# Layer 3's weight products placed behind layer 2's experts, and the first expert's matrices issued ahead of its rows

## The chip, the cores and the metric

The kernel runs on one core of one Trainium2 chip. The metric is the time of one execution on the device, in microseconds (us). Five engines work side by side, each through its own queue of instructions in order: TensorE (PE), VectorE (DVE), ScalarE (ACT), GpSimd (POOL) and SyncE (SP). SP and ACT also issue plain DMA transfers, POOL the indirect ones.

## The reference, cut to what matters

The program is a stack of four hybrid layers on an image of 256 channels and 64 x 64 pixels. Layers 0 and 1 are convolutional. Layers 2 and 3 work on 4096 tokens of 256 numbers; each is an attention and then a mixture of 8 experts, of which each token uses the two that its router ranks highest:

```python
def _L2_ffn_ref(input_embeddings, router_w, w1, b1, w2, b2):      # hidden size 256
    ...
            logits = tokens.astype(jnp.float32) @ router_w.astype(jnp.float32).T
            probs = jax.nn.softmax(logits, axis=-1)
            rw, re = jax.lax.top_k(probs, TOP_K)
    ...
            for e in range(E):
                h = jax.nn.gelu(tokens @ w1[e] + b1[e], approximate=False)
                y = h @ w2[e] + b2[e]
                out = out + combine[:, e:e + 1] * y
def _L3_attn_ref(x, Wq, bq, Wk, bk, Wv, bv):
    Q = jnp.einsum('bsd,de->bse', x, Wq) + bq
    K = ...
    V = jnp.einsum('bsd,de->bse', x, Wv) + bv
    scores = jnp.einsum('bqd,bkd->bqk', Q, K) * scale
    weights = jax.nn.softmax(scores, axis=-1)
    return jnp.einsum('bqk,bkd->bqd', weights, V)
def _L3_ffn_ref(x, Wg, bg, W1, b1, W2, b2):                       # hidden size 1024
    ...
        out = out + w_dense[:, e:e + 1] * (h @ W2[e] + b2[e])

t = _to_tokens(x)
t = t + _L2_attn_ref(_ln_t(t), ...)
t = t + _L2_ffn_ref(_ln_t(t), ...)
t = t + _L3_attn_ref(_ln_t(t), ...)
t = t + _L3_ffn_ref(_ln_t(t), ...)
```

## The kernel before, in words

The tokens stay in one SBUF array `t`, 128 partitions by 32 tiles of 256. `run` (L2465) calls `attn2`, `attn3`, `experts` and `store` in turn, each layer's expert stage in three steps:

- `route` (L1771) takes a block of four tiles. It normalizes the tokens into `n` (for layer 2 it also writes the normalized tokens, added to `t`, back into `t`: L1783, and four activations on ACT, L1785), turns `n` over on PE in two halves (k = 0 is copied by ACT, k = 1 by DVE, L1792), multiplies by the router's matrix, picks the best two experts (`top2`), counts how many rows each expert has so far, and writes every token's row to its expert's place in the DRAM array `xs` by eight indirect scatters on POOL (L1828). It is a generator: the attention's loop runs it piece by piece between its own blocks, and the last of the eight blocks is routed after the attention's end. In layer 2 `n` lies in attention's array `a_qk`, in layer 3 in `f_room`.
- `tile_table` (L1835) works out on DVE, from the counts, which expert each tile of 256 rows belongs to and at which row of `xs` it starts. It ends in the table `tab`, from which SP reads a register for the expert (row 0 of the table) and one for the first row (row 1).
- `experts` (L1889) runs `expert_tiles` (L1906) over 36 tiles, and over three more only if they are needed. `load(i)` reads the two registers and issues three DMAs on SP: the rows `f_x` (L1919, 260 KB), and the expert's matrices `f_w1` (L1921) and `f_w2` (L1923), together 0.65 MB in layer 2 and 2.2 MB in layer 3. Loads run three tiles ahead in layer 2, two in layer 3. `turn` (L1926) turns the rows over on PE and copies them to `f_xT` on DVE (L1932). `first` (L1936) multiplies by `w1` and applies Gelu on ACT (L1942). `where` (L1945) is nine DVE operations on two numbers per partition (L1950 to L1958) that find where each row's result goes and its weight. In layer 3 `sides` combines parts of `w2` on POOL into `f_wt` (L1969), and `seven` (L1972) forms the second product from seven smaller ones, with sums `f_hs` of DVE. `second` (L2001) scatters the results to the DRAM array `ys` by two indirect scatters on POOL (L2012).

Layer 3's attention needs three matrices that are products of its weights: `wvp` (one subtraction on DVE, L2119), `wqk` (PE, copied at L2124) and `bqk` (PE, copied at L2127). `attn3` (L2092) loads the weights for them into a pool of their own, `weights3` (three DMAs, L124, two on SP and one on ACT's queue), computes the products, and only then calls `self.experts(S)` for layer 2:

```python
self.weights(wpool, ["w_qkT3", "w_v3p", "w_v3s"])
nc.vector.tensor_tensor(wvp, w["w_v3p"], w["w_v3s"], ALU.subtract)
...
self.experts(S)
```

After that, its `add(b)` (L2144) fetches two results per token from `ys` (`outputs`, L2040) and adds them to `t` on DVE (L2151), and the attention starts.

The library's scheduler orders each engine's instructions by a model of their times and may move one ahead of others that were written earlier. Inside `tc.manual_schedule(engines=...)` the named engines keep the written order: PE in layer 2's attention loop, PE and POOL in layer 3's, whose `tile_table` is in the same block. Buffers come from pools; a pool that opens on memory which an earlier one used makes its writers wait for the earlier use to end.

Of the kernel before, what the change touches and what calls it, by code (L numbers as in the profile page):

```python
# [10 lines left out]
F32 = mybir.dt.float32  # L11
BF16 = mybir.dt.bfloat16
I32 = mybir.dt.int32
AF = mybir.ActivationFunctionType
ALU = mybir.AluOpType
# [73 lines left out]
class Net:  # L89
# [1088 lines left out]
    def attn2(self, t, S):  # L1178

        nc, tc = self.nc, self.tc  # L1180
        with tc.tile_pool(name="a2", bufs=1) as pool:
            A = {}
            A["qk"] = pool.tile([P, NT, 2 * C], F32, tag="qk", name="a2_qk")
            A["v"] = pool.tile([P, NT, C], F32, tag="v", name="a2_v")
            A["vT"] = pool.tile([P, 2, N], F32, tag="vT", name="a2_vT")

            for nm in ("sim", "gate", "fac"):
                A[nm] = pool.tile([P, 2, NT // 2, NH], F32, tag=nm, name=f"a2_{nm}")
            wg_bd = pool.tile([P, 2, P], F32, tag="wg_bd", name="wg_bd")
            self.kv_blocks(pool, None, wg_bd)  # L1190

            ked = pool.tile([P, 2, D], F32, tag="ked", name="a2_ked")
            nc.sync.dma_start(out=ked, in_=self.A["kvn_ed"].rearrange("(m p d) -> p m d", p=P, d=D))
            dif = pool.tile([P, 2, D], F32, tag="dif", name="a2_dif")
            nc.vector.tensor_tensor(dif, ked, bc(ked[:, :, 0], 2, D), ALU.not_equal)
            nc.vector.tensor_reduce(self.flags[:, 1:2], dif.rearrange("p m d -> p (m d)"), AX.X, ALU.max)
            with (
                tc.tile_pool(name="a2w", bufs=2) as wp,
                tc.tile_pool(name="a2_ps", bufs=2, space=PSUM) as ps,
            ):  # L1200
                self.rows(wp, "b_qkv2", "b_qkv2")


                stages = [self.attn2_project(b, t, A, wg_bd, wp, ps) for b in range(NBLK)]
                go = lambda b, *names: [stages[b][nm]() for nm in names if 0 <= b < NBLK]
                with tc.manual_schedule(engines={mybir.EngineType.PE}):
                    go(0, "norm", "turn")
                    for b in range(-1, NBLK):
                        go(b + 2, "norm")
                        go(b + 1, 0)  # L1210
                        go(b, "turn_v", "lengths")
                        go(b + 1, 1, 2)
                        go(b, "sims")
                        go(b + 1, 3)
                        go(b + 2, "turn")
                        go(b, "gates")
            self.attn2_fac(A)
            with (
                tc.tile_pool(name="a2x", bufs=2) as wp,
                tc.tile_pool(name="a2x_ps", bufs=1, space=PSUM) as ps,  # L1220
            ):
                bank = lambda: ps.tile([P, NB], F32, tag="r", name="f_r_ps")

                def route(t0, T):

                    n = A["qk"][:, t0 : t0 + T, :].rearrange("p t c -> p (t c)")[:, : T * CX]
                    nT = A["v"][:, t0 : t0 + T, :].rearrange("p t c -> p (t c)").rearrange("p (a n) -> p a n", a=2)
                    return self.route(t0, T, t, S, wp, n.rearrange("p (i c) -> p i c", c=CX), nT, bank)

                self.attn2_sum(t, A, ked, wp, ps, route)  # L1230
            with (
                tc.tile_pool(name="a2t", bufs=1) as wp,
                tc.tile_pool(name="a2t_ps", bufs=1, space=PSUM) as ps,
            ):
                self.tile_table(S, wp, lambda: ps.tile([P, NB], F32, tag="r", name="f_r_ps"))

    def kv_blocks(self, pool, kv_bd, wg_bd):

# [532 lines left out]
    def route(self, t0, T, t, S, wp, n, nT, bank):  # L1771
# [6 lines left out]
        small = lambda p: p[:, : T * NE].rearrange("p (i e) -> p i e", e=NE)  # L1778
        flat = lambda a: a.rearrange("p i e -> p (i e)")
        r, shift = self.layer_norm(wp, t[:, tiles, :], n[:, :, :C], 1e-5, on_act=(L == 2))  # L1780
        if L == 2:

            nc.vector.tensor_scalar_add(r, r, 1.0)  # L1783
            for i in range(T):
                nc.scalar.activation(t[:, t0 + i, :], t[:, t0 + i, :], AF.Identity, bias=shift[:, i : i + 1], scale=r[:, i : i + 1])  # L1785
        nc.gpsimd.tensor_copy(n[:, :, C], self.out_row[:, tiles])
        yield
        for k in range(2):
# [1 line left out]
            for i in range(T):  # L1790
                nc.tensor.transpose(p[:, i * P : (i + 1) * P], n[:, i, k * P : (k + 1) * P], self.ident)
            (nc.scalar.copy, nc.vector.tensor_copy)[k](nT[:, k, :], p[:, : T * P])  # L1792
            yield
        p = small(bank())
        for i in range(T):
            self.mm(p[:, i, :], [(nT[:, kt, i * P : (i + 1) * P], wr[:, kt, :]) for kt in range(2)])
# [37 lines left out]
    def tile_table(self, S, wp, bank):  # L1834
# [6 lines left out]

        ci = tl([NE], "ci", I32)
        nc.vector.tensor_copy(ci, c_ps)
        rows = tl([NE], "rows")
        nc.vector.tensor_copy(rows, c_ps)
        nc.vector.tensor_single_scalar(ci, ci, MT - 1, ALU.add)
        nc.vector.tensor_single_scalar(ci, ci, MT.bit_length() - 1, ALU.arith_shift_right)
        cnt = tl([NE], "cnt")
        nc.vector.tensor_copy(cnt, ci)
        ends = tl([NE], "ends")  # L1850
        nc.vector.tensor_copy(ends[:, 0:1], cnt[:, 0:1])
        for e in range(1, NE):
            nc.vector.tensor_add(ends[:, e : e + 1], ends[:, e - 1 : e], cnt[:, e : e + 1])

        last = tl([1], "last")
        nc.vector.tensor_scalar_add(last, ends[:, NE - 1 : NE], -1.0)
# [3 lines left out]
        nc.vector.tensor_tensor(past, bc(ends, 1, NTILE), bc(tau, 2, NE), ALU.is_le)  # L1860
        ex = S["ex"]
        nc.vector.tensor_reduce(ex, past, AX.X, ALU.add)
        nc.vector.tensor_tensor(past, past, bc(cnt, 1, NTILE), ALU.mult)
        skip = tl([NTILE], "skip")
        nc.vector.tensor_reduce(skip, past, AX.X, ALU.add)
        nc.vector.tensor_sub(tau, tau, skip)
        nc.vector.tensor_scalar_mul(tau, tau, float(MT))
        nc.vector.scalar_tensor_tensor(skip, ex, float(N), tau, ALU.mult, ALU.add)
        tab = S["tab"]
        nc.vector.tensor_scalar_mul(tab[:, 0, :], ex, float(P))  # L1870
        nc.vector.tensor_copy(tab[:, 1, :], skip)
        nc.vector.tensor_copy(S["used"], ends[:, NE - 1 : NE])

        nc.vector.tensor_tensor(past, bc(ex, 2, NE), bc(self.count[:, :NE], 1, NTILE), ALU.is_equal)
# [30 lines left out]
    def expert_tiles(self, S, tiles, wp, ps):  # L1905
# [7 lines left out]
        def load(i):  # L1913
# [2 lines left out]
            row = nc.values_load(tab[0:1, 1, i : i + 1], engines=[mybir.EngineType.SP], min_val=0, max_val=NE * N - MT,  # L1916
                                 skip_runtime_bounds_check_because=why)
            x = wp.tile([P, NI, CX], F32, tag="x", name="f_x", bufs=ahead + 3)
            nc.sync.dma_start(out=x, in_=self.xs[bass.ds(row, MT), :].rearrange("(i p) c -> p i c", p=P))  # L1919
            w1 = wp.tile([P, 2 * hidden + KH], F32, tag="w1", name="f_w1")  # L1920
            nc.sync.dma_start(out=w1, in_=A[f"f{L}_w1"][bass.ds(e, P), :])  # L1921
            w2 = wp.tile([P, KH * C + C], F32, tag="w2", name="f_w2")
            nc.sync.dma_start(out=w2, in_=A[f"f{L}_w2"][bass.ds(e, P), :])  # L1923
            return x, w1, w2

        def turn(x):  # L1926
# [88 lines left out]
                )  # L2015

        tiles = list(tiles)
        ld = {i: load(i) for i in tiles[:ahead]}
        xT = turn(ld[tiles[0]][0])
        to = where(tiles[0], ld[tiles[0]][0])  # L2020
# [72 lines left out]
    def attn3(self, t, S):  # L2093
# [6 lines left out]
        with (  # L2100
# [10 lines left out]
            wqk = pool.tile([P, 2, C], F32, tag="wqk", name="a3_wqk")  # L2111
            bqk = pool.tile([P, 2], F32, tag="bqk", name="a3_bqk")
            wvp = pool.tile([P, 2, C + 1], F32, tag="wvp", name="a3_wvp")
            with (
                tc.tile_pool(name="weights3", bufs=1) as wpool,
                tc.tile_pool(name="a3m_ps", bufs=1, space=PSUM) as ps,
            ):
                self.weights(wpool, ["w_qkT3", "w_v3p", "w_v3s"])
                nc.vector.tensor_tensor(wvp, w["w_v3p"], w["w_v3s"], ALU.subtract)  # L2119
                wT = w["w_qkT3"]  # L2120
                for m in range(2):
# [3 lines left out]
                    p = ps.tile([P, 1], F32, tag=f"b{m}", name="a3_b_ps")  # L2125
                    self.mm(p, [(wT[:, kt, C + m * P : C + (m + 1) * P], self.par("bq3", kt)) for kt in range(2)])
                    nc.vector.tensor_copy(bqk[:, m : m + 1], p)  # L2127
            self.experts(S)
            with (
                tc.tile_pool(name="a3w", bufs=2) as wp,  # L2130
                tc.tile_pool(name="a3_ps", bufs=1, space=PSUM) as ps,
# [223 lines left out]
                with tc.manual_schedule(engines={ET.PE, ET.Pool}):  # L2355
# [19 lines left out]
                        finish(NBLK - 1, i)  # L2375
                    for _ in route((NBLK - 1) * TPB, TPB):
                        pass
                    self.tile_table(S, wp, bank)

    def limits3(self, S, pool):  # L2380
# [253 lines left out]
```

## Time and profile before

| | |
|---|---|
| time | 3632.52 us, median of 3 runs (3632.32 to 3634.52) |
| profiled run | 3632.83 us, span 3631.1 us, mean granted TensorE clock 0.964 |
| busy share of the span | PE 91%, DVE 64%, POOL 45%, ACT 39% |
| layer 2's experts | first row load 1962.23 us, last product on PE ends 2134.7, last scatter lands 2140.7 |
| layer 3's experts | first row load 3071.45 us, last scatter lands 3585.8, then the store to the end |

A busy share is an average over the whole span. The chain of work that ended last runs through PE for 36% of the span, DVE 8%, DMA 5%. Times in the text are microseconds from the span's start. In a line of the timeline the columns are start, duration, engine, line of the kernel, operation, output and input by the program's names, sizes, count, and in brackets how long the engine was idle before and what released it. SPq and ACTq are the DMA instructions of these engines' queues.

### The profile page before, as it was taken

The page shows a single profiled execution, that of the slowest core. Times are in us where ns is not written, and L with a number is a line of the kernel's source. Part 1 is how long each engine was busy: PE and PEld are TensorE (multiplying, and loading weights), DVE is VectorE, ACT ScalarE, POOL GpSimd, SP SyncE. Part 2 cuts the span into 40 slices and gives each one's busy share as a digit, 9 for nine tenths or more (in the row PEclk, how much of TensorE's full clock was granted, in tenths as well). Part 3 has the DMA queues.
Part 4 walks back from the last instruction along what each step waited for, and adds up shares of the span by engine and source line. Part 5 has one row for each costly group of instructions (what it writes and reads, how often), then busy time and mean ns, then how long its engine had stood idle before and what let it go on. Part 6 is the DMA issues. An engine that isn't in the chain of part 4 may idle for free.

```text
span 3631.1 us, 62669 instructions
## 1 busy us (share of the span) xinstructions
PE 3319.8 (91%) x23572; PEld 2360.4 (65%) x23572; DVE 2340.0 (64%) x5678; ACT 1413.7 (39%) x2891; POOL 1640.0 (45%) x1587
## 2 busy tenths in 40 slices
PE   6989999999999678979796969999999997999997
PEld 4443434334333478876585746888888886898986
DVE  6756656656566367778775557677777776555552
ACT  5544344343443366634252335222222222333331
POOL 1028889888888155544343435200000002555552
PEclk9999999999999889989896989999999998999998
DMA  1002424401001612220014865333222332555554
GB/s 59 3 29 83 132 58 119 142 22 42 33 25 36 185 50 72 75 63 1 1 59 153 259 216 188 105 99 99 93 93 93 99 94 95 193 212 190 208 198 181
DMA packets 160703, 377.44 MB, mean 104 GB/s; under 512 B 17345, under 2 KB 75458, under 8 KB 151170
## 3 DMA queue, kind: packets, MB, share of 16 engines
q1 hardware_dynamic: 136162, 317.91, 27.1%
q0 software_dynamic: 13056, 35.93, 2.6%
q10 hardware_dynamic: 11168, 19.42, 1.5%
q8 instruction: 192, 3.15, 0.4%
q14 instruction: 125, 1.02, 0.1%
HBM read 273.44 MB, written 99.76 MB: 103 GB/s over the span
## 4 chain that ended last, share of the span: by engine, by line
PE 36%; DVE 8%; DMA 5%; issue 5%; POOL 3%; ACT 2%; SPq 0%; POOLq 0%; ACTq 0%; DVEq 0%
PE a_sa_ps L2258 5%; PE f_h_ps L146 5%; DMA ys<-f_y,f_at 3%; PE a_oa_ps L2297 3%; PE a_ob_ps L2297 3%; PE a_oc_ps L2297 3%; PE a_sb_ps L2258 2%; PE f_ya_ps L146 2%; PE f_yb_ps L146 2%; POOL ys L2012 1%; PE l_acc_ps L957 1%; PE a_od_ps L2297 1%; PE a_q_ps L146 1%; PE a_sc_ps L2258 1%; PE a_o_ps L146 1%
## 5 line engine op out<-in xcount | busy, mean ns | idle before, releaser
L584 POOL TENSOR_TENSOR l_sm<-l_sc,mask 128x512 f32<-128x512 f32 (+3 forms) x624 | 770.2, 1273 | 118.7 <-ACT l_sc L574 116.3
L578 DVE TENSOR_TENSOR l_sm<-l_s,mask 128x256 f32<-128x256 f32 (+3 forms) x1248 | 491.9, 447 | 300.8 <-PE l_s L568 291.1
L574 ACT COPY l_sc<-l_s 128x384 f32<-128x384 f32 (+3 forms) x896 | 367.8, 461 | 557.8 <-PE l_s L568 540.5
L568 PE MATMUL l_s<-l_q,l_k 32*128 32x384 f32 (+2 forms) x3584 | 425.3, 514 | 7.4 <-ACT l_sc L574 4.1
L1828 POOL DMA_INDIRECT xs<-f_room,f_to x64 | 64.4, 1007 | 697.1 <-issue 582.3
L146 PE MATMUL f_h_ps<-f_xT,f_w 128*128 128x256 f32 x1440 | 342.8, 388 | 20.6 <-DVE f_xT L1932 9.7
L568 PEld LDWEIGHTS l_s<-l_q,l_k 32*128 32x128 f32 x3584 | 165.5, 183 | 241.9 <-issue 124.7
L146 PEld LDWEIGHTS f_h_ps<-f_xT,f_w 128*128 128x128 f32 x1440 | 262.1, 192 | 86.4 <-ACT f_h L1942 31.0
L2277 ACT ACTIVATE a_e<-a_e 128x512 f32<-128x512 f32 x256 | 155.9, 629 | 242.8 <-DVE a_e L2247 239.4
L1942 ACT ACTIVATE f_h<-f_h_ps,f_w 128x256 f32<-128x256 f32 x360 | 166.3, 470 | 170.0 <-PE f_h_ps L146 170.0
L953 DVE TENSOR_TENSOR l_pr<-l_vk,l_w_ps 128x1280 f32<-128x1280 f32 x128 | 186.5, 1480 | 55.4 <-PE l_acc_ps L957 37.4
L2012 POOL DMA_INDIRECT ys<-f_y,f_at x144 | 145.5, 1011 | 149.4 <-ACT f_y L2011 89.6
L957 PE MATMUL l_acc_ps<-ident,l_pr 128*128 128x128 f32 x1600 | 197.1, 277 | 9.4 <-POOL l_pr L948 9.2
L957 PEld LDWEIGHTS l_acc_ps<-ident,l_pr 128*128 128x128 f32 x1600 | 183.6, 143 | 15.9 <-POOL l_pr L948 11.1
L1969 POOL TENSOR_TENSOR f_wt<-f_w 128x512 f32<-128x512 f32 x72 | 90.0, 1271 | 211.9 <-PE f_ya_ps L146 200.0
L611 PE MATMUL l_a_ps<-l_sm,l_v 128*32 128x512 f32 (+3 forms) x1408 | 178.7, 530 | 1.1 <-POOL l_sm L584 1.0
L611 PE MATMUL l_b_ps<-l_sm,l_v 128*32 128x256 f32 (+2 forms) x2176 | 171.5, 376 | 0.5 <-POOL l_sm L584 0.5
L2258 PE MATMUL a_sa_ps<-a_q,a_kt 128*128 128x256 f32 x512 | 156.1, 387 | 13.5 <-DVE a_u L2263 12.6
L2262 ACT COPY a_u<-a_sa_ps 128x256 f32<-128x256 f32 x128 | 47.6, 372 | 293.1 <-PE a_sa_ps L2258 293.1
L2258 PE MATMUL a_sa_ps<-a_qt,a_kt 128*128 128x256 f32 x512 | 152.7, 380 | 0.0
L2297 PE MATMUL a_ob_ps<-a_et,a_vs 128*128 128x256 f32 x512 | 131.4, 379 | 0.0
L2258 PE MATMUL a_sb_ps<-a_qt,a_kt 128*128 128x256 f32 x512 | 131.4, 379 | 0.0
(533 smaller groups left out, 6843.5 us busy)
## 6 DMA issues: line engine op xcount, KB each, us to landing
a_kt<-a_kd SPq DMA_DIRECT2D x128, 512.0 KB
f_w<-in_f_w SPq DMA_DIRECT2D x36, 1152.0 KB
f_w<-in_f_w SPq DMA_DIRECT2D x36, 1028.0 KB
xs<-zero SPq DMA_DIRECT2D x8, 4160.0 KB
l_vk<-vt SPq DMA_DIRECT2D x180, 128.0 KB
f_x<-xs SPq DMA_DIRECT2D x72, 260.0 KB
f_w<-in_f_w SPq DMA_DIRECT2D x36, 384.0 KB
l_rcp<-l_recd SPq DMA_DIRECT2D x48, 256.0 KB
```

The source lines that it names most:

```text
L146: self.nc.tensor.matmul(out, lhsT, rhs, start=(i == 0), stop=(i == len(pairs) - 1))
L568: nc.tensor.matmul(s[pair, j], k[hp, key * P : (key + 1) * P], qs[hp], start=True, stop=True)
L574: nc.scalar.copy(sc[:, j], s[1, j])
L578: nc.vector.tensor_tensor(sms[0][:, j, at : at + t * wide].rearrange("p (t n) -> p t n", n=wide), part[:, which, :], mask, ALU.mult)
L584: nc.gpsimd.tensor_tensor(sms[1][:, :, at : at + t * wide].rearrange("p j (t n) -> p j t n", n=wide), part[:, :, which, :], bc(mask, 1, 2) ...
L611: nc.tensor.matmul(out, v[:, key, hp], sms[pair][:, j, base + lo * wide : base + hi * wide], start=not seen[nm], stop=(left[nm] == 0 and h ...
L953: nc.vector.tensor_tensor(pr, vk, bc(held["w"][:, j, dy], 3, D), ALU.mult)
L957: nc.tensor.matmul(acc[:, m, j, :], pf[:, dx, m * P : (m + 1) * P], self.ident, is_transpose=True, start=(j == 0 and dy == 0 and dx == 0 a ...
L1942: nc.scalar.activation(h[:, m, :], q, AF.Gelu, bias=w1[:, 2 * hidden + m : 2 * hidden + m + 1])
L2012: nc.gpsimd.indirect_dma_start(out=self.ys_parts[(i % 4) * NI + k], in_=y[:, k, :], in_offset=None, out_offset=bass.IndirectOffsetOnAxis(a ...
L2258: mm = lambda out, i, right: nc.tensor.matmul(out, A[i], right, start=True, stop=True)
L2297: nc.tensor.matmul(out, vs[:, j, i, :], right, start=(j == 0 and side != 1), stop=(j == NPAIR - 1 and side != 0))
```

## The change

It has six parts. In `attn3` layer 2's experts now come ahead of the loads and products of layer 3's weights, whose buffers lie in the pool `a3` instead of `weights3`. In `load`, for the first tile alone, the two matrices are issued ahead of the rows. In `route`, for layer 2, the operation L1783 and the four activations L1785 stand after the second copy of the turned tokens instead of ahead of the first; the number of pieces stays the same. `tile_table` runs in written order on DVE, in layer 2 in a block of its own for DVE, in layer 3 in one of its own for PE, POOL and DVE. In it a scan takes the place of a copy and seven additions, the table's first row is written sooner, and the copy `rows` stands later. `expert_tiles` begins with a Gelu of one column into a buffer `f_gelu` that nothing reads.

```diff
@@ -1232,7 +1232,8 @@
                 tc.tile_pool(name="a2t", bufs=1) as wp,
                 tc.tile_pool(name="a2t_ps", bufs=1, space=PSUM) as ps,
             ):
-                self.tile_table(S, wp, lambda: ps.tile([P, NB], F32, tag="r", name="f_r_ps"))
+                with tc.manual_schedule(engines={mybir.EngineType.DVE}):
+                    self.tile_table(S, wp, lambda: ps.tile([P, NB], F32, tag="r", name="f_r_ps"))
 
     def kv_blocks(self, pool, kv_bd, wg_bd):
 
@@ -1778,11 +1779,6 @@
         small = lambda p: p[:, : T * NE].rearrange("p (i e) -> p i e", e=NE)
         flat = lambda a: a.rearrange("p i e -> p (i e)")
         r, shift = self.layer_norm(wp, t[:, tiles, :], n[:, :, :C], 1e-5, on_act=(L == 2))
-        if L == 2:
-
-            nc.vector.tensor_scalar_add(r, r, 1.0)
-            for i in range(T):
-                nc.scalar.activation(t[:, t0 + i, :], t[:, t0 + i, :], AF.Identity, bias=shift[:, i : i + 1], scale=r[:, i : i + 1])
         nc.gpsimd.tensor_copy(n[:, :, C], self.out_row[:, tiles])
         yield
         for k in range(2):
@@ -1790,7 +1786,14 @@
             for i in range(T):
                 nc.tensor.transpose(p[:, i * P : (i + 1) * P], n[:, i, k * P : (k + 1) * P], self.ident)
             (nc.scalar.copy, nc.vector.tensor_copy)[k](nT[:, k, :], p[:, : T * P])
-            yield
+            if k == 0:
+                yield
+        if L == 2:
+
+            nc.vector.tensor_scalar_add(r, r, 1.0)
+            for i in range(T):
+                nc.scalar.activation(t[:, t0 + i, :], t[:, t0 + i, :], AF.Identity, bias=shift[:, i : i + 1], scale=r[:, i : i + 1])
+        yield
         p = small(bank())
         for i in range(T):
             self.mm(p[:, i, :], [(nT[:, kt, i * P : (i + 1) * P], wr[:, kt, :]) for kt in range(2)])
@@ -1841,16 +1844,12 @@
 
         ci = tl([NE], "ci", I32)
         nc.vector.tensor_copy(ci, c_ps)
-        rows = tl([NE], "rows")
-        nc.vector.tensor_copy(rows, c_ps)
         nc.vector.tensor_single_scalar(ci, ci, MT - 1, ALU.add)
         nc.vector.tensor_single_scalar(ci, ci, MT.bit_length() - 1, ALU.arith_shift_right)
         cnt = tl([NE], "cnt")
         nc.vector.tensor_copy(cnt, ci)
         ends = tl([NE], "ends")
-        nc.vector.tensor_copy(ends[:, 0:1], cnt[:, 0:1])
-        for e in range(1, NE):
-            nc.vector.tensor_add(ends[:, e : e + 1], ends[:, e - 1 : e], cnt[:, e : e + 1])
+        nc.vector.tensor_tensor_scan(ends, self.one.to_broadcast([P, NE]), cnt, 0.0, ALU.mult, ALU.add)
 
         last = tl([1], "last")
         nc.vector.tensor_scalar_add(last, ends[:, NE - 1 : NE], -1.0)
@@ -1860,15 +1859,17 @@
         nc.vector.tensor_tensor(past, bc(ends, 1, NTILE), bc(tau, 2, NE), ALU.is_le)
         ex = S["ex"]
         nc.vector.tensor_reduce(ex, past, AX.X, ALU.add)
+        tab = S["tab"]
+        nc.vector.tensor_scalar_mul(tab[:, 0, :], ex, float(P))
         nc.vector.tensor_tensor(past, past, bc(cnt, 1, NTILE), ALU.mult)
         skip = tl([NTILE], "skip")
         nc.vector.tensor_reduce(skip, past, AX.X, ALU.add)
         nc.vector.tensor_sub(tau, tau, skip)
         nc.vector.tensor_scalar_mul(tau, tau, float(MT))
         nc.vector.scalar_tensor_tensor(skip, ex, float(N), tau, ALU.mult, ALU.add)
-        tab = S["tab"]
-        nc.vector.tensor_scalar_mul(tab[:, 0, :], ex, float(P))
         nc.vector.tensor_copy(tab[:, 1, :], skip)
+        rows = tl([NE], "rows")
+        nc.vector.tensor_copy(rows, c_ps)
         nc.vector.tensor_copy(S["used"], ends[:, NE - 1 : NE])
 
         nc.vector.tensor_tensor(past, bc(ex, 2, NE), bc(self.count[:, :NE], 1, NTILE), ALU.is_equal)
@@ -1916,11 +1917,16 @@
             row = nc.values_load(tab[0:1, 1, i : i + 1], engines=[mybir.EngineType.SP], min_val=0, max_val=NE * N - MT,
                                  skip_runtime_bounds_check_because=why)
             x = wp.tile([P, NI, CX], F32, tag="x", name="f_x", bufs=ahead + 3)
-            nc.sync.dma_start(out=x, in_=self.xs[bass.ds(row, MT), :].rearrange("(i p) c -> p i c", p=P))
+            rows = lambda: nc.sync.dma_start(out=x, in_=self.xs[bass.ds(row, MT), :].rearrange("(i p) c -> p i c", p=P))
+
+            if i > 0:
+                rows()
             w1 = wp.tile([P, 2 * hidden + KH], F32, tag="w1", name="f_w1")
             nc.sync.dma_start(out=w1, in_=A[f"f{L}_w1"][bass.ds(e, P), :])
             w2 = wp.tile([P, KH * C + C], F32, tag="w2", name="f_w2")
             nc.sync.dma_start(out=w2, in_=A[f"f{L}_w2"][bass.ds(e, P), :])
+            if i == 0:
+                rows()
             return x, w1, w2
 
         def turn(x):
@@ -2015,6 +2021,8 @@
                 )
 
         tiles = list(tiles)
+
+        nc.scalar.activation(wp.tile([P, 1], F32, tag="g", name="f_gelu", bufs=1), self.one, AF.Gelu)
         ld = {i: load(i) for i in tiles[:ahead]}
         xT = turn(ld[tiles[0]][0])
         to = where(tiles[0], ld[tiles[0]][0])
@@ -2111,11 +2119,9 @@
             wqk = pool.tile([P, 2, C], F32, tag="wqk", name="a3_wqk")
             bqk = pool.tile([P, 2], F32, tag="bqk", name="a3_bqk")
             wvp = pool.tile([P, 2, C + 1], F32, tag="wvp", name="a3_wvp")
-            with (
-                tc.tile_pool(name="weights3", bufs=1) as wpool,
-                tc.tile_pool(name="a3m_ps", bufs=1, space=PSUM) as ps,
-            ):
-                self.weights(wpool, ["w_qkT3", "w_v3p", "w_v3s"])
+            self.experts(S)
+            with tc.tile_pool(name="a3m_ps", bufs=1, space=PSUM) as ps:
+                self.weights(pool, ["w_qkT3", "w_v3p", "w_v3s"])
                 nc.vector.tensor_tensor(wvp, w["w_v3p"], w["w_v3s"], ALU.subtract)
                 wT = w["w_qkT3"]
                 for m in range(2):
@@ -2125,7 +2131,6 @@
                     p = ps.tile([P, 1], F32, tag=f"b{m}", name="a3_b_ps")
                     self.mm(p, [(wT[:, kt, C + m * P : C + (m + 1) * P], self.par("bq3", kt)) for kt in range(2)])
                     nc.vector.tensor_copy(bqk[:, m : m + 1], p)
-            self.experts(S)
             with (
                 tc.tile_pool(name="a3w", bufs=2) as wp,
                 tc.tile_pool(name="a3_ps", bufs=1, space=PSUM) as ps,
@@ -2375,6 +2380,7 @@
                         finish(NBLK - 1, i)
                     for _ in route((NBLK - 1) * TPB, TPB):
                         pass
+                with tc.manual_schedule(engines={ET.PE, ET.Pool, ET.DVE}):
                     self.tile_table(S, wp, bank)
 
     def limits3(self, S, pool):
```

## The prediction, as it was put on record before the change was run

> **What bounds the kernel now.** I read the engine shares first (TensorE, PE, is busy 91% of the span), then the windows by stage, then the timeline of the two places that the diff touches: the borders at which a layer's routing ends and its experts begin. The windows (columns: us of the stretch, then busy us of PE, its weight loads, DVE, ACT and POOL, then granted clock, DMA share, GB/s):
>
> ```profile
> 1950.00:1962.00 12.00, 5.05 (x16) 4.37 (x16) 1.69 (x4) 0.00 (x0) 0.14 (x1) 0.50 0.30 99
> 1962.00:2140.00 178.00, 157.77 (x721) 122.55 (x721) 89.64 (x398) 64.20 (x145) 69.09 (x72) 0.96 0.76 240
> 2134.00:2154.00 20.00, 1.03 (x5) 0.42 (x3) 9.15 (x22) 4.07 (x9) 3.84 (x4) 0.65 0.51 188
> 3072.00:3090.00 18.00, 11.69 (x44) 9.37 (x45) 10.91 (x22) 4.97 (x9) 8.55 (x7) 0.72 0.98 382
> 3090.00:3555.00 465.00, 460.41 (x3082) 419.50 (x3081) 258.16 (x675) 161.02 (x371) 250.70 (x200) 1.00 0.55 198
> ```
>
> Inside both expert stages PE is nearly full, so a stage ends later or earlier by as much as its first expert tile does. Only the borders can be shortened, and PE's hole from 2134 to 2154 is free room. Layer 2's border, on SP's queue (start, duration):
>
> ```profile
> 1952.10 0.37 SPq L124 DMA_DIRECT2D w_qkT<-in_w_qkT  x1
> 1952.52 0.46 SPq L124 DMA_DIRECT2D w_v3s<-in_w_v3s  x1
> 1962.23 0.40 SPq L1919 DMA_DIRECT2D f_x<-xs  x1
> 1963.16 0.35 SPq L1921 DMA_DIRECT2D f_w<-in_f_w  x1
> 1963.70 0.35 SPq L1923 DMA_DIRECT2D f_w<-in_f_w  x1
> 1964.56 0.39 SPq L1919 DMA_DIRECT2D f_x<-xs  x1
> ```
>
> Ten us pass in which only layer 3's weight products run; SP's wait list puts 4.0 us of the wait at L1919 down to their last matmul. The last scatter (1949.18) lands at 1951.60, which releases 1952.10. Before it, ACT holds up the routing:
>
> ```profile
> 1925.99 2.07 ACT L1785 ACTIVATE t<-t,ln_shift,ln_rstd 128x256 f32<-128x256 f32 x4 [0.24 <-DVE ln_rstd L1783]
> 1927.96 0.56 ACT L1792 COPY a_v<-f_r_ps 128x512 f32<-128x512 f32 x1
> ```
>
> Layer 3's border, PE, then DVE and POOL:
>
> ```profile
> 3077.44 8.56 PE L146 MATMUL f_h_ps<-f_xT,f_w 128*128 128x256 f32 x28 [1.97 <-DMA f_w<-in_f_w]
> 3089.66 7.17 PE L146 MATMUL f_h_ps<-f_xT,f_w 128*128 128x256 f32 x32 [1.96 <-DVE f_xT L1932]
> ```
> ```profile
> 3074.47 0.23 DVE L1950 TENSOR_SCALAR f_first<-f_x,f_ex 128x2 f32<-128x2 f32 x1 [6.95 <-DMA f_x<-xs]
> ...
> 3080.87 1.31 DVE L1950 TENSOR_SCALAR f_first<-f_x,f_ex 128x2 f32<-128x2 f32 x1 [4.38 <-DMA f_x<-xs]
> 3082.21 1.19 DVE L1951 TENSOR_SCALAR f_second<-f_first 128x2 f32<-128x2 f32 x1
> ...
> 3088.93 0.68 DVE L1932 COPY f_xT<-f_x_ps 128x512 f32<-128x512 f32 x1
> ```
> ```profile
> 3080.89 2.49 POOL L1969 TENSOR_TENSOR f_wt<-f_w 128x512 f32<-128x512 f32 x2 [11.39 <-DMA f_x<-xs]
> ```
>
> The same tiny DVE operation takes 0.23 us alone and 1.31 while POOL combines weights. That is what delays tile 1's f_xT, and with it PE, to 3089.66.
>
> **What the Trainium skill says.** "DMA: Bandwidth & Descriptors", Queues, rings and completion order: descriptors of a queue are taken in ring order on each DMA engine. The trace agrees: layer 3's second rows, issued at 3073.73 behind 2.2 MB of matrices, land after 7.11 us, the first rows after about 2.7. "GPSIMD Engine Reference", Key points: GpSimd shares its SBUF interfaces with VectorE, which contends in 2-port modes or with two SBUF inputs; the 0.23 against 1.31 above agrees. "ScalarE: Activation LUTs", What ACT_TABLE_LOAD costs: about 1283 ns for a table; here 1.28 at 3079.63, and it starts after f_h's products, so it is beside PE's work.
>
> **The change part by part.**
>
> *Weight products moved behind layer 2's experts.* The first expert load takes w_qkT's place: 1952.10 instead of 1962.23, -10.1. Its register loads are ready (the table's last row is written at 1945.64). What moves: three DMAs (two on SP, one on ACT's queue, 1.03 MB), PE's products (cold, 1956.95 to 1962.20, 5.3 us), five DVE operations (0.69 + 2 x 0.42 + 2 x 0.16 = 1.9 us); nothing on POOL. They fall into 2135 to 2153.65, where PE waits for attn3's first a_vs, DVE is free until 2145.23 and SP issues no DMA between 2117.5 and 2141.28. I take 0. Bounds: below, -1 (PE a little warmer for attn3); above, +10.8, if the loads start only when the last outputs land: 4.9 (w_v3p's issue to the first product) + 5.3 + 0.6 of copies, with attn3's adds queued behind these copies on DVE.
>
> *Four ACTs and r+1 moved behind the k=1 copy (layer 2).* Block 7's a_v copy starts when its transposes end (1925.80 + 0.48 = 1926.28), not at 1927.96: -1.7, down the chain transposes, router, top-2 to the scatters; POOL stands idle 3.57 us ahead of these, so all eight move. The moved 2.07 us of ACT lie beside the router's work; the next ACT operation is due at 1936.19. In the other blocks PE is full, which hides the same edit: 0. Bounds -2.0 to -0.8.
>
> *Matrices ahead of rows, first tile.* The reading on which most rests: expert buffers can't be filled before the last scatter has landed, since w_qkT and w_v3p, fresh buffers with no use for xs, both waited for exactly that (the releaser on SP's list is xs). So the matrices get no head start worth the name; the rows queue behind them. Layer 2: issued 1.40 later (1963.16 to 1964.56), and x(1) took 3.87 us to land behind 0.65 MB where x(0) took 2.7; I take +2.1 (bounds +1.4 to +2.6). Queued behind the rows on SP are tile 1's loads, at the place they had. Layer 3: 260 + 1028 + 1152 + 260 KB landed by 3080.84, one row tile fewer at 382 GB/s by 3080.1, where x(0) now lands near 3074.2. By then w2(0) is there too, and POOL starts f_wt(0), so tile 0's nine small DVE operations now meet what tile 1's met. If f_xT follows five of them (layer 2's order): 3.95 us (3080.87 to about 3084.8) and 0.69 of copy, f_h(0) at 3084.75. If it follows all nine: until f_wt(0)'s 5.1 us end, plus some 0.5 and 0.69: 3086.4. Tile 0 holds PE for 10.26 us (3077.44 to 3087.70), so f_h(1) starts at 3095.0 or 3096.7 instead of 3089.66: +5.3 or +7.0; I take +6.2. Without the meeting: f_h(0) 2.3 after the rows, 3082.4, f_h(1) +3.0. So the bounds are +3.0 and +8.5 (x(0) 1.5 later).
>
> *Tile table in written order, scan, early Gelu.* A scan of 8x16 costs 0.18 here (L1387) and replaces eight operations of 0.16 to 0.2, under eight scatters at 1.27 us pitch: 0. In layer 3 f_rows leaves the way of f_to: -0.3 (-0.5 to +0.3). The Gelu load: 0, as above; its output is a fresh expert buffer, so ACT waits there for the scatters, and queued behind it is only the first f_h, which comes later anyway.
>
> *Sum.* Layer 2: -10.1 - 1.7 + 2.1 = -9.7. Layer 3: +6.2 - 0.3 = +5.9. Together -3.8, against a span of 3631.1 whose run took 3632.83; the other runs are 3632.32 and 3634.52, so from the median 3632.52 I get 3628.7.
>
> **Rivals.** 0.2% (7.3 us) is about what a measurement of this kernel can tell from no change.
>
> A, 0.47: the sum above, -6 to 0; about 3628.7.
>
> B, 0.22: rows and f_wt don't meet (DVE gets in first, or POOL later). Layer 3 loses 3.0 - 0.3; total -7.0, with layer 2's bounds -9 to -5: 3625.5. For: POOL and DVE started within 0.02 us of each other at 3080.88, so a little shift decides. Against: DVE needs nine instructions.
>
> C, 0.17: matrices do come ahead of the scatters' landing (another memory region). Then the rows keep their issue: layer 2 -11.8, layer 3 gains f_h(0)'s 0.9 beyond f_xT and part of tile 1's, about -2: 3618. For: f_cum, also a fresh buffer, is written at 2140.02, a shade before the last outputs land at 2140.70. Against: w_qkT.
>
> D, 0.14, slower: the products are not hidden. If the weight loads wait at 2141 for the last outputs and attn3's first adds stand behind the copies on DVE, up to +10.8 comes on the critical path; with -3.8 that is +7.0, 3639.5. It decides from +3.8 on. For: other fresh buffers waited so. Against: SP and ACT are free from 2137 and these buffers lie where nothing of the experts is.
>
> That the change doesn't do what it says applies to the early matrices alone, and A is that case.
>
> **How the numbers follow.** Time: A's. A's own range is 3625 to 3633. The range must reach C (3618, with its bounds 3615.5) and most of D: 3615.5 to 3639.5. Faster by over 0.2%: C, half of B and the lower end of A (0.17 + 0.11 + 0.14) 0.42; slower by over 0.2%: half of D and 0.04 of A for what I overlook, 0.11; between, 0.47.
>
> **What would show it.** Right: first f_w on SP near 1950.4, f_x third; first f_h near 1957; a_w_ps inside 2135 to 2153; in layer 3 f_h(0) near 3085 less layer 2's 9.7, with L1950 of tile 0 above 1 us. Wrong: f_w issued before the last scatter lands (C), tile 0's L1950 at 0.23 (B), attn3's first add more than 9 us behind the last f_y's scatter (D; now 6.89 from 2138.34). If layer 2's experts don't start some 10 us earlier, my first step fails and with it everything.

## The result, and the profile after

The changed kernel took 3620.2 us (median of 4 runs, 3617.91 to 3626.44) against 3633.52 before (4 runs, 3632.32 to 3637.23): ratio 0.9964, 95% interval 0.9947 to 0.9982, so 13 us less. Single times scatter by 3 us and more, and two later comparisons with more runs, told below, gave 0.9978 (0.997 to 0.9986) and 0.9976 (0.9967 to 0.9985): by these ratios 8.1 and 8.7 us less. The change is faster, by 8 to 13 us. The forecast was 3.8 less, with "no clear change" as the likeliest case. The measured time lies inside the stated range, but outside rival A's own range (3625 to 3633): the range reached so low only to take in rival C, which didn't happen.

The profiled run of the changed kernel took 3626.44 (span 3624.6), and is 2.6 us later than before already at `a_seg`, in the middle of layer 2's attention, ahead of everything that the diff touches. So I compare stretches between fixed points, not readings of the clock. Layer 2's border, SP's queue after (start, duration):

```profile
1953.08 0.38 SPq L1925 DMA_DIRECT2D f_w<-in_f_w  x1
1953.67 0.35 SPq L1927 DMA_DIRECT2D f_w<-in_f_w  x1
1954.56 1.28 SPq L1920 DMA_DIRECT2D f_x<-xs  x2
```

The last scatter was issued at 1950.14, the first matrix 2.94 us later, where before 13.05 us passed until the first rows. The matrices didn't get ahead of the scatters' landing. Tile 0's rows are third, and tile 1's follow at once (x2). ACT in block 7's routing after:

```profile
1928.52 0.60 ACT L1795 ACTIVATE t<-t,ln_shift,ln_rstd 128x256 f32<-128x256 f32 x1 [0.24 <-DVE ln_rstd L1793]
1929.02 0.56 ACT L1788 COPY a_v<-f_r_ps 128x512 f32<-128x512 f32 x1
1929.49 1.58 ACT L1795 ACTIVATE t<-t,ln_shift,ln_rstd 128x256 f32<-128x256 f32 x3
```

One of the four activations is still ahead of the a_v copy, three are behind it. The weight products on PE after, then PE's next work:

```profile
2126.92 1.13 PE L146 MATMUL a_w_ps<-w_qkT 128*128 128x256 f32 x4 [2.13 <-ACTq L1903]
2127.88 0.50 PE L146 MATMUL a_b_ps<-pp,w_qkT 128*128 128x1 f32 x4
2128.25 1.11 PE L146 MATMUL a_w_ps<-w_qkT 128*128 128x256 f32 x4
2129.19 0.50 PE L146 MATMUL a_b_ps<-pp,w_qkT 128*128 128x1 f32 x4
2144.16 2.81 PE L2186 MATMUL a_q_ps<-ident,a_vs 128*128 128x128 f32 x8 [14.46 <-ACT a_vs L2176]
```

They take 2.8 us at a granted clock of 1.00, where they took 5.3 at 0.50 before, and 14.5 us of idle PE follow: hidden on PE, as forecast. Their loads went out among layer 2's experts (w_qkT at 2085.0; w_v3p, on ACT's queue, already at 1953.09). On DVE they are not quite free. Attention 3's first adds, before and then after:

```profile
2145.23 2.49 DVE L2151 TENSOR_TENSOR t<-t,f_room 128x1024 f32<-128x1024 f32 x2 [5.14 <-DMA f_room<-ys]
```
```profile
2135.46 1.23 DVE L2156 TENSOR_TENSOR t<-t,f_room 128x1024 f32<-128x1024 f32 x1 [4.37 <-DMA f_room<-ys]
2136.61 0.42 DVE L2130 COPY a_wqk<-a_w_ps 128x256 f32<-128x256 f32 x1
2136.94 0.15 DVE L2133 COPY a_bqk<-a_b_ps 128x1 f32<-128x1 f32 x1
2137.00 1.22 DVE L2156 TENSOR_TENSOR t<-t,f_room 128x1024 f32<-128x1024 f32 x1
```

Two copies of the products stand between the adds. Attention 3's first product on PE (`a_q_ps`) starts 19.3 us after layer 2's last f_y, where it was 18.9 before.

Layer 3's border after, first DVE, then POOL, then PE:

```profile
3071.92 1.09 DVE L1956 TENSOR_SCALAR f_first<-f_x,f_ex 128x2 f32<-128x2 f32 x1 [14.60 <-DMA f_x<-xs]
3073.05 1.19 DVE L1957 TENSOR_SCALAR f_second<-f_first 128x2 f32<-128x2 f32 x1
3074.27 0.16 DVE L1958 TENSOR_TENSOR f_wgt<-f_second,f_x 128x2 f32<-128x2 f32 x1
3074.35 1.23 DVE L1963 TENSOR_TENSOR f_first<-f_first,f_x 128x2 f32<-128x2 f32 x1
...
3076.18 0.68 DVE L1938 COPY f_xT<-f_x_ps 128x512 f32<-128x512 f32 x1
```
```profile
3070.51 2.48 POOL L1975 TENSOR_TENSOR f_wt<-f_w 128x512 f32<-128x512 f32 x2 [9.87 <-DMA f_w<-in_f_w]
3072.96 2.60 POOL L1975 TENSOR_TENSOR f_wt<-f_w,f_wt 128x512 f32<-128x512 f32 x2
```
```profile
3071.25 1.94 PE L1936 MATMUL f_x_ps<-ident,f_x 128*128 128x128 f32 x8 [22.43 <-DMA f_x<-xs]
3076.91 16.18 PE L146 MATMUL f_h_ps<-f_xT,f_w 128*128 128x256 f32 x64 [3.72 <-DVE f_xT L1938]
```

Tile 0's first small operation takes 1.09 us beside POOL's sums, where it took 0.23 before: the meeting that the forecast rested on. The slow operations end where a sum of POOL ends: at 3073.01, 3074.24 and 3075.58, POOL's first pair at 3072.99, its second at 3075.56. So each of them costs about what is left of one sum of 1.25 us, and the others in the queue run at their usual 0.15 to 0.23. In the other profiles that have slow ones it is the same, within 0.04 us. The copy f_xT follows eleven small operations (nine of tile 0, two of tile 1), where the forecast had five or nine. PE turned over both tiles at once (x8), and f_h(0) and f_h(1) run without a break (x64).

The stretches, in us, of profiles from chips on which the kernel before takes about 3630 us. f_h is a layer's first expert product on PE (f_h(0) that of tile 0), f_y the sum on DVE that ends a tile; "order" means the matrices ahead of the rows. Each column is one execution, so a difference of 2 to 3 us between two columns can be scatter:

| stretch | before | route only | order only | products only | changed | changed (3rd) | rows first | rows first (2nd) |
|---|---|---|---|---|---|---|---|---|
| a_seg (start of the attention's second part) to last scatter | 189.6 | 187.8 | 189.2 | 190.4 | 187.9 | 187.9 | 187.6 | 187.9 |
| to the first load of the experts | 13.0 | 13.0 | 13.0 | 3.0 | 2.9 | 3.0 | 3.1 | 3.1 |
| to f_h, layer 2 | 4.7 | 4.8 | 6.9 | 6.0 | 7.7 | 7.8 | 6.0 | 6.1 |
| to layer 2's last f_y | 167.8 | 165.5 | 162.9 | 170.8 | 164.0 | 161.6 | 164.2 | 166.2 |
| to layer 3's last scatter | 933.8 | 933.5 | 933.1 | 935.2 | 934.8 | 934.4 | 933.8 | 934.3 |
| to f_h, layer 3 | 8.9 | 10.7 | 17.2 | 10.7 | 17.2 | 17.1 | 10.4 | 10.4 |
| to layer 3's last f_y | 503.2 | 505.3 | 499.7 | 501.9 | 498.7 | 498.5 | 501.0 | 509.3 |
| to the end | 50.5 | 50.2 | 49.9 | 49.8 | 49.0 | 47.8 | 48.9 | 47.7 |

### The profile page after: what moved, and what is told of

Its sections match the earlier page's. It is cut to its first block, busy times and chain, and to the rows that moved or that the text cites. A ratio compares the mean times of both kernels' runs of the same rounds, so it can differ in the third digit from the quotient of the medians.

```text
span 3624.6 us, 62648 instructions
## 1 busy us (share of the span) xinstructions
PE 3315.4 (91%) x23572; PEld 2358.9 (65%) x23572; DVE 2332.7 (64%) x5664; ACT 1414.6 (39%) x2893; POOL 1640.0 (45%) x1587
## 3 DMA queue, kind: packets, MB, share of 16 engines
q14 instruction: 124, 1.02, 0.1%
## 4 chain that ended last, share of the span: by engine, by line
PE 36%; DVE 7%; issue 5%; DMA 5%; POOL 3%; ACT 2%; SPq 0%; POOLq 0%; DVEq 0%; ACTq 0%
PE a_sa_ps L2263 5%; PE f_h_ps L146 5%; PE a_oa_ps L2302 3%; PE a_ob_ps L2302 3%; DMA ys<-f_y,f_at 3%; PE a_oc_ps L2302 3%; PE a_sb_ps L2263 3%; PE f_ya_ps L146 2%; PE f_yb_ps L146 2%; POOL ys L2018 1%; PE a_od_ps L2302 1%; PE a_q_ps L146 1%; PE a_sc_ps L2263 1%; PE l_acc_ps L957 1%; PE a_o_ps L146 1%
```

## The experiments

Theory 1 is the forecast's sum by parts. Its rival after the first comparison, theory 2, was that the order of the loads had brought the unforecast gain. e1 to e12 are the runs; each was measured against the kernel before on the same chip.

**Rows first again in the changed kernel (e1).**

```diff
-            if i > 0:
-                rows()
+            rows()
...
-            if i == 0:
-                rows()
```

> The changed kernel with the rows ahead of the matrices again for the first tile. Theory 1 (in layer 3 the matrices-first order makes the first tile's DVE operations meet POOL's weight sums, which costs 5 us; in layer 2 it costs 1 to 2): 6 us less than the changed kernel, about 17 to 19 us less than before, layer 3's first f_h about 8 us sooner after the last scatter. Theory 2 (the order is what brought the unforecast part of the gain, because two tiles then run back to back): 3 to 8 us more than the changed kernel, 5 to 10 less than before.

Measured: 3622.93 against 3630.19 before, ratio 0.9979 (0.997 to 0.9988), 7.3 us less. Layer 3's f_h starts 10.4 us after the last scatter instead of 17.2, as theory 1 has it. The time is no better than the changed kernel's, which speaks for theory 2, but the two were not in the same group; so the pair was repeated (e9, e10).

**The order alone (e2).** The kernel before, with the loads of the change:

```diff
-            nc.sync.dma_start(out=x, in_=...)
+            rows = lambda: nc.sync.dma_start(out=x, in_=...)
+            if i > 0:
+                rows()
...
+            if i == 0:
+                rows()
```

> The kernel before, with the matrices ahead of the rows for the first tile and nothing else. Theory 1: 6 us more than before, with tile 0's L1950 above 1 us in layer 3 and f_h(0) some 8 us later. Theory 2: 3 to 8 us less than before.

Measured: 3634.36, ratio 1.001 (1.0002 to 1.0018), 4.2 us more: theory 1's sign, and less than its 6. The table shows why it is less: layer 2's f_h comes 2.2 us later (4.7 to 6.9), and the rest of that stage is 4.9 shorter.

**The products alone (e3).**

```diff
+            self.experts(S)
-            with (
-                tc.tile_pool(name="weights3", bufs=1) as wpool,
-                tc.tile_pool(name="a3m_ps", bufs=1, space=PSUM) as ps,
-            ):
-                self.weights(wpool, ["w_qkT3", "w_v3p", "w_v3s"])
+            with tc.tile_pool(name="a3m_ps", bufs=1, space=PSUM) as ps:
+                self.weights(pool, ["w_qkT3", "w_v3p", "w_v3s"])
...
-            self.experts(S)
```

> The kernel before with layer 3's weight products moved behind layer 2's experts and nothing else. Theory 1: the first row load takes w_qkT's place, 10.1 us sooner, and layer 2's experts end 10 us sooner; 9 to 12 us less than before. Theory 2: not more than 6 us less, the rest being due to the order of the loads.

Measured: 3622.57, ratio 0.9979 (0.9971 to 0.9988), 7.6 us less. The first load comes the forecast 10 us sooner after the last scatter (3.0 against 13.0). Layer 2's f_h then takes 1.3 us longer from that load, and the stage is 3 us longer than before's in this profile. Theory 2's bound of 6 us is exceeded, but the interval of the gain (4.4 to 10.5 us) reaches below it.

**The route alone (e4).** L1783 and L1785 moved, the rest as before:

```diff
-        if L == 2:
-            nc.vector.tensor_scalar_add(r, r, 1.0)
-            for i in range(T):
-                nc.scalar.activation(...)
...
+            if k == 0:
+                yield
+        if L == 2:
+            ...
+        yield
```

> The kernel before with L1783 and the four activations L1785 moved behind the second copy, nothing else. Theory 1: 1.6 us less (last scatter of layer 2 that much sooner), which is at the edge of what can be measured. Rival: the loop of layer 2's attention gains as well in each of its eight blocks, 5 us or more less.

Measured: 3629.7, ratio 0.9998 (0.999 to 1.0006). The time can't tell 1.6 us from nothing; the traces can: 187.8 against 189.6 to the last scatter, 187.6 to 188.6 in six profiles of other versions with the edit (after, e1, e9 to e12), 189.2 and 190.4 in the two others without it (e2, e3). The rival (5 us or more) falls.

**The changed kernel again (e5), without an edit.**

> The changed kernel once more, with more runs. Theory 1 (the parts add up: products moved -7.6, loads' order +4.2, route -0.5, the rest nothing): 4 us less than before (2 to 7), the first comparison having been lucky with four runs whose single times scatter by 3 us. Theory 2 (together the parts bring more than apart, because two tiles start back to back): 9 us less or more, as first measured.

Measured on another chip: 3688.49 against 3696.0, ratio 0.9978 (0.997 to 0.9986), 7.5 us by the medians. That lies between the two theories' figures. The parts add to 7.6 - 4.2 + 0.5 = 3.9 less, and together they are worth twice that, though the intervals of the three parts (3 us each way) leave room.

**POOL's sums held back (e6).**

```diff
+            if hold is not None:
+                nc.vector.tensor_copy(wt[:, 0, 0, 0:1], hold[:, 0, 0:1])
...
-            now = (i, h, w2, sides(w2)) + to
+            now = (i, h, w2, sides(w2, xT if i == tiles[0] else None)) + to
```

> The changed kernel with POOL's weight sums of the first tile held until f_xT of that tile is copied (one DVE copy of a number into f_wt makes POOL wait). Theory 1 (POOL's sums slow tile 0's small DVE operations): these go back from 1.1 to 0.16 us, layer 3's f_h(0) starts 2.7 us sooner after its rows have landed, and the time is about 2.7 us below the changed kernel's. Rival (the operations are slow because the DMA engines write SBUF at full rate): they stay above 1 us and nothing is gained.

One of the four sums, which doesn't depend on the held one, still ran ahead of the rows' landing. Measured: 3684.63, ratio 0.9972 (0.9958 to 0.9986), 3.9 us below e5's median, with overlapping intervals. DVE and PE of layer 3's start:

```profile
3133.23 0.23 DVE L1956 TENSOR_SCALAR f_first<-f_x,f_ex 128x2 f32<-128x2 f32 x1 [14.69 <-DMA f_x<-xs]
3133.50 0.17 DVE L1957 TENSOR_SCALAR f_second<-f_first 128x2 f32<-128x2 f32 x1
...
3134.58 0.68 DVE L1938 COPY f_xT<-f_x_ps 128x512 f32<-128x512 f32 x1
```
```profile
3135.32 16.11 PE L146 MATMUL f_h_ps<-f_xT,f_w 128*128 128x256 f32 x64 [0.82 <-DVE f_xT L1938]
```

The DMA engines are as busy as in e5 (share 1.04 against 1.02) and the operations are back at 0.23 and 0.17: it was POOL. From first operation to copy 1.35 us instead of 4.28 (3131.55 to 3135.83 in e5); f_h 14.4 after the last scatter instead of 17.0. The rival falls. This is what the Trainium skill's "GPSIMD Engine Reference", Key points, leads one to expect (interfaces to SBUF shared with VectorE); the copy from PSUM took 0.68 in either case. Of the 2.5 us by which f_h comes sooner, 1.2 are left at layer 3's last f_y (513.7 us after the last scatter, against 514.9).

**Rows of both tiles ahead of w2 (e7).**

```diff
+            x, w1 = get_x(row), get_w1(e)
+            f, row = regs(j)
+            z = get_x(row)
+            w2 = get_w2(e)
...
+        ld = load_two(*tiles[:2])
```

> The changed kernel with another order of the first loads: rows of tile 0, its w1, rows of tile 1, its w2, then tile 1's matrices. Theory 1: both tiles' small DVE operations lie ahead of w2's landing and so of POOL's sums; layer 3's f_h(0) waits for w1 alone and f_h(1) follows it without a gap: 7 us below the changed kernel, 1 to 3 below the version with the rows first. Rival (tile 0's start is set by w1's landing in any order): not more than 3 us below the changed kernel.

Measured: 3682.99, ratio 0.9961 (0.9947 to 0.9975), 5.5 us below e5's median. Layer 3's f_h waits for w1 (10.7 after the last scatter, against 10.4 with the rows first), and f_h(1) only 0.52 for its f_xT. The waits are as theory 1 has them. The time is nearer to its 7 than to the rival's 3, but it is from five runs and the intervals of the two ratios overlap. The stretch from layer 3's last scatter to its last f_y is 3.6 us shorter than in e5 (511.3 against 514.9), that in layer 2 is 2.3 longer (176.2 against 173.9).

**All weight loads on SP (e8).**

```diff
-                self.weights(pool, ["w_qkT3", "w_v3p", "w_v3s"])
+                for name in ("w_qkT3", "w_v3p", "w_v3s"):
+                    self.weights(pool, [name])
```

> The changed kernel with all three weight loads on SP's queue, so that w_v3p isn't issued on ACT's queue at the moment in which the first expert's loads are. Theory 1 (its 257 KB share the DMA engines with the first rows): layer 2's first f_h 1.3 us sooner after the first load's issue (7.7 to 6.4), time 1 us lower, at the edge of what can be told. Rival: no difference in the trace.

Measured: 3687.63, ratio 0.9978 (0.9969 to 0.9988). From the first load to f_h in layer 2 it takes 7.64 us against 7.79 in e5. The rival holds with this order of the loads. With the rows first it is 5.23 with all weights on SP (e11) against 6.04 and 6.05 without (e1, e10), so there w_v3p costs 0.8 us.

**The changed kernel and the rows first, side by side (e9, e10, no new edit).**

> The changed kernel for a direct comparison with the others of this group: 8 us less than before (7 to 9), as the second comparison gave.

> The changed kernel with the rows ahead of the matrices for the first tile, beside the changed kernel itself. Theory (from the traces: layer 3's experts take 4 us less from last scatter to last f_y, layer 2's 1 less): 5 us less than the changed kernel, 13 less than before. Rival (from the times: the first group gave -7.3 for it, no better than the changed kernel): within 2 us of the changed kernel.

Measured against 3633.49 before: 3623.82, ratio 0.9976 (0.9967 to 0.9985), as expected, and 3621.43, ratio 0.997 (0.9959 to 0.998). Rows first is 2.4 us better by the medians, with overlapping intervals: nearer the rival. What the order of the loads is worth in the changed kernel isn't settled by this; in the kernel before, matrices first cost 4.2 us (e2). PE at the start of layer 3 in e10:

```profile
3067.19 9.30 PE L146 MATMUL f_h_ps<-f_xT,f_w 128*128 128x256 f32 x32 [3.60 <-DMA f_w<-in_f_w]
...
3082.52 10.17 PE L146 MATMUL f_h_ps<-f_xT,f_w 128*128 128x256 f32 x32 [4.03 <-DVE f_xT L1935]
```

With the rows first f_h(0) starts 6.7 us sooner after the scatters, but tile 1's f_xT is what then meets POOL's sums, and f_h(1) waits 4.03 us here (1.51 in e1, 1.96 before). After that wait f_h(1) runs 10.17 us instead of 7.17, at a mean granted clock of 0.69. The Trainium skill's "TensorE: Matmul & The Clock Gate", What's actually happening, says that PE drops to half its clock after an idle window of about 3.4 us; 4.03 us of idle with 10.17, and 1.51 and 1.96 with 7.17, agree with it; the 2.55 us of e4, after which f_h(1) took 8.86 with a clock of 0.51 for part of it, are shorter than that window.

**Rows first in layer 2, both rows in layer 3, weights on SP (e11).** The edits of e1, e7 (for layer 3 alone) and e8 together.

> Rows first in layer 2; in layer 3 rows of tile 0, its w1, rows of tile 1, its w2; all three weight loads on SP. Theory: layer 2's first f_h 4.7 us after its first load instead of 6.0 (w_v3p no longer beside the first rows), layer 3 as with both rows first: 6 to 7 us less than the changed kernel, 14 to 15 less than before, the fastest version. Rival: layer 2's first f_h stays at 6.0, and the time is that of the version with the rows first.

Measured: 3619.34, ratio 0.9963 (0.995 to 0.9976), 4.5 us below e9's median: the lowest median of its group, a little short of the 6 to 7, from five runs and with intervals that overlap. PE:

```profile
3066.30 8.95 PE L146 MATMUL f_h_ps<-f_xT,f_w 128*128 128x256 f32 x32 [2.91 <-DMA f_w<-in_f_w]
...
3077.35 7.17 PE L146 MATMUL f_h_ps<-f_xT,f_w 128*128 128x256 f32 x32
```

No wait is left before f_h(1), and layer 3's stage from last scatter to last f_y takes 511.2 us (changed: 515.9 and 515.5). Layer 2's takes 177.1 (changed: 174.7 and 172.4), so in these single profiles most of that is lost again there.

**The table and the early Gelu undone (e12).**

```diff
-                with tc.manual_schedule(engines={mybir.EngineType.DVE}):
...
-        nc.vector.tensor_tensor_scan(ends, ...)
+        nc.vector.tensor_copy(ends[:, 0:1], cnt[:, 0:1])
+        for e in range(1, NE):
+            nc.vector.tensor_add(...)
...
-        nc.scalar.activation(wp.tile([P, 1], F32, tag="g", name="f_gelu", bufs=1), self.one, AF.Gelu)
```

> The changed kernel without its three small parts (tile table in the scheduler's order again, with copy and additions instead of the scan and no early Gelu). Theory: these lie under the eight scatters and beside PE's work: within 1 us of the changed kernel. Rival (the early Gelu takes a table load out of the first tile): 1.3 us or more above the changed kernel in each layer.

Measured: 3623.96, ratio 0.9976 (0.9969 to 0.9984), against 3623.82 in e9: no difference, as forecast, though the intervals leave room for 2 to 3 us. The trace decides against the rival: without the early Gelu the table load ends at 1953.79 in layer 2, 4.9 us ahead of the first Gelu, and in layer 3 it starts at 3073.04, while f_h's products run on PE.

## Why the prediction was right in sign and small in size

*Products moved: right.* The first load comes 10.1 us sooner, and the products lie in PE's hole. Two small costs stand where the forecast took 0. w_v3p, on ACT's queue, went out at the very moment of the first expert loads (0.8 us with the rows first, e11; 0.15 with the matrices first, e8). And the copies of the products delay attention 3: its first product comes 19.0 to 19.7 us after layer 2's last f_y in the profiles with the products moved, 18.9 in the three without. Rival D, the products on the path, didn't happen: the loads didn't wait for the results, and attention 3's first add starts 7.0 us behind the last f_y's scatter (6.89 before; D wanted more than 9).

*Route: right.* Forecast -1.7, traces -1.8.

*Matrices wait for the scatters too: right.* First f_w 2.94 us after the last scatter's issue; rival C, by which they come ahead, falls.

*Layer 2, "I take +2.1": wrong.* The delay of f_h is there (+2.2 in e2, +1.7 from e1 to changed), but the stage doesn't end later by it. From the first load to the last f_y it takes 168.8 to 171.8 us in the seven profiles with the matrices first and 170.3 to 176.8 in the seven with the rows first. The means are 2.6 us apart, the nearest pairs 0.7 (after and e9 against e1 and e10) and 1.6 (e2 against before and e4). So no loss, and a gain of 1 to 3 us whose size single profiles don't settle. The step that failed is "a stage ends later or earlier by as much as its first expert tile does", for want of idle time on PE: the line it was read from has PE busy for 157.77 of 178.00 us, which leaves 20. I followed tile 0 alone. Before, tile 1 had a wait of its own, seen on PE:

```profile
1966.91 2.08 PE L146 MATMUL f_h_ps<-f_xT,f_w 128*128 128x256 f32 x4 [0.78 <-DVE f_xT L1932]
1968.78 1.06 PE L1930 MATMUL f_x_ps<-ident,f_x 128*128 128x128 f32 x4
1970.62 3.78 PE L146 MATMUL f_h_ps<-f_xT,f_w 128*128 128x256 f32 x8 [0.78 <-DVE f_xT L1932]
```

After, both tiles' rows land together and their products run in one piece:

```profile
1960.79 5.80 PE L146 MATMUL f_h_ps<-f_xT,f_w 128*128 128x256 f32 x16
```

From f_h to PE's first product for f_y it took 8.1 us before and takes 6.1 changed. But PE's clock has a part in this, and it differs between executions: of the same eight products after tile 1's transposes, the line above has 3.78 us (granted clock 0.50 from 1965 to 1975), the profile of e4, with the same order of loads, 1.99 (clock 1.00):

```profile
1964.55 1.99 PE L146 MATMUL f_h_ps<-f_xT,f_w 128*128 128x256 f32 x8 [0.78 <-DVE f_xT L1934]
```

The changed kernel shows both cases as well (5.80 us for the sixteen above, 4.34 in e5). So part of the 2.0 is luck of the profile and not the order.

The rest of the stage is shorter too: from f_h to the last f_y 161.2 to 164.0 us in the seven profiles with the matrices first, 164.2 to 170.8 in the seven with the rows first. From PE's wait list in that stretch, changed (e9), then rows first (e10), with columns total us, times, longest:

```profile
PE f_h_ps L146 <- ACT f_h L1948: 4.1, 15, 0.7
PE f_h_ps L146 <- DVE f_xT L1938: 3.3, 5, 1.5
```
```profile
PE f_h_ps L146 <- DVE f_xT L1935: 6.2, 8, 1.6
PE f_h_ps L146 <- ACT f_h L1945: 6.1, 17, 1.0
```

In all fourteen profiles PE's waits for f_xT come to 2.8 to 6.2 us with the matrices first and 6.0 to 10.0 with the rows first. f_xT is late where it stands behind f_at on DVE, which waits for an earlier tile's results to land, here in the profile of the changed kernel:

```profile
2100.39 0.16 DVE L1962 TENSOR_TENSOR f_at<-f_to,f_off 128x2 int32<-128x2 f32 x1 [2.48 <-DMA ys<-f_y,f_at]
...
2100.80 0.69 DVE L1938 COPY f_xT<-f_x_ps 128x512 f32<-128x512 f32 x1
```

DVE's waits for these results come to 50 to 61 us and are no shorter with the matrices first, so not their sum but what stands behind them would make the difference, and the order of the first loads changes the scheduler's sequence. That it does so through this queue is argued, not shown, and no run here settles it. Together: +2 at the start and some -4.5 in the rest by the means, so near -2.5 where the sum has +2.1.

*Layer 3, "I take +6.2": right mechanism, too large.* f_h(0) was forecast 16.2 or 17.9 us after the last scatter (3084.75 or 3086.4 less 3068.53), and measured at 17.2. Two terms were mis-sized. "Tile 0 holds PE for 10.26 us": that time held tile 1's transposes and a piece of tile 0's second product, which now lie elsewhere; both tiles take 16.18, so tile 0 some 9.1. That puts f_h(1) 5.2 us later than before, and f_h(2) is 5.3 later (3099.61 less 3059.67 against 3103.14 less 3068.53), as the lower of the two forecasts had it. But the end of the stage doesn't move by as much: from f_h(2) to the last f_y it takes 476.0 us instead of 477.5. From last scatter to last f_y 515.9 and 515.5 stand against 512.1 (before): +3.4 to +3.8. The profile before was a good one, though. The five with the rows first (before, e1, e3, e4, e10) have 511.4 to 519.7, by the length of f_h(1)'s wait (1.51 to 4.03), and 514.4 in the mean; the six with the matrices first (after, e2, e5, e8, e9, e12) have 514.9 to 518.2, and 516.5. Against the mean it is +2.1.

*Small parts: right*, as far as e12 can tell.

With the terms as measured the sum is -10.1 + 0.8 (w_v3p) - 1.8 - 2.5 + 3.7 + 0.4 (copies) = -9.5, near the 8.1, 8.7 and 13 measured. It is an estimate: with 0.15 for w_v3p (e8) and +2.1 for layer 3 it is -11.8. What remains, another 0.2 to 0.6 us between the experts (933.8 before, 934.8 and 934.4 changed, less the 0.4) and 1.5 to 2.7 less at the end (50.5 before, 49.0 and 47.8 changed), I can't tell from scatter. The surest part is the move of the products, which alone gave 7.6 us (e3).

As far as these profiles show, the forecast came out too small because it took both expert stages to follow their first tile.

## What to carry to other kernels

Before you let a stage's end follow its first tile, look how much idle time its busiest engine has: a late start can be made up there. A transfer that is moved behind others delays its own tile, but look one tile further: if the next tile's data then comes with it, a wait of that tile may go. Where small operations of one engine are slow beside big ones of another (1.1 to 1.3 us instead of 0.15 to 0.23 here), ask which small operations in an in-order queue stand in front of the one that counts, and keep the big operations away from just these (here the rows of both tiles ahead of the matrix that sets POOL off, e7 and e11). Compare a version of two parts with both parts alone, and more than four runs, before adding effects of a few us.

## What the runs showed that I had not expected

- Layer 2's attention, from a_seg to the last scatter, takes 188 us on one chip and 252 on another, with the same instructions, at a granted clock of 0.86 against 0.78 in that stretch (changed kernel, 1762 to 1950, and e5, 1756 to 2008). That is 64 of the 65 us between the medians of e5 and e9. Why the chips differ there is open.
- A wait of 2.55 us before f_h(1) (e4) goes with 8.86 us for it, between the 7.17 after 1.5 to 2 us and the 10.17 after 4.03.
